# A later input load and held second-layer steps at the start of the deformable layers

## The chip, the cores and the metric

The kernel runs on one core of a Trainium2 chip. The metric is the device time of one execution in microseconds, as the median of runs: 5149.69 us, of three runs between 5146.34 and 5154.36 us. A separate execution was taken by the hardware profiler; all durations in this document come from such executions.

The core has five engines that follow their own lists of instructions in order: TensorE (PE in the profile), VectorE (DVE), ScalarE (ACT), GpSimd (POOL) and SyncE (SP). They wait for each other by semaphores only. POOL and SP also issue DMA transfers, each on a queue of its own.

## The reference, cut to what matters

Four layers follow each other on an input of 2 images, 256 channels, 64 x 64 pixels, in float32:

```python
x = group_norm(x) + proj(attention(group_norm(x)))   # layer 0: four heads over 4096 pixels
x = x + position_term                                # layer 1
h = relu(bn(conv1x1(x)))                             # layer 2: 256 -> 64 channels
h = relu(bn(deform_conv(h)))                         #   3x3 taps, offsets and masks from h
x = relu(bn(conv1x1(h)) + x)                         #   64 -> 256 channels
h = deform_conv(relu(group_norm(x)))                 # layer 3: two deformable 3x3 convolutions
x = deform_conv(relu(group_norm(h))) + x             #   of 256 channels, offsets from h
```

A deformable convolution reads, for each output pixel and each of its nine taps, four neighbouring pixels at an address that was computed from the data, weights them, and multiplies the sum with the weights of the tap:

```python
samp = gather(y0, x0) * w00 + gather(y0, x0+1) * w01 + gather(y0+1, x0) * w10 + gather(y0+1, x0+1) * w11
out = einsum('bckhw,ock->bohw', samp, w)
```

## The kernel before, in words

The program has two functions that follow each other. `attention` computes layers 0 and 1 and, between the products of the attention, layer 2 of the first image and the beginning of the rest. `deform` computes what is left: layer 2 of the second image, and layer 3 of both.

**An image in memory.** Before it is sampled, an image is written to memory by pixels, two rows side by side, so that one row of it holds two neighbouring pixels of two lines, and two such rows, read as one, hold the four neighbours of a sample. A gather (`gather`, line 844) is an indirect DMA on POOL's queue: 128 addresses, one for each partition, from a table of indices in SBUF.

**The main loop of `deform`.** Layer 3 has four passes: two convolutions of two images. Each pass has eight blocks of 512 pixels, each block nine taps of four groups of 128 pixels. A sample `s` is one tap of one group: 36 samples in a block (`BLOCK`), 288 in a pass, 1152 in all. The loop runs over `s` and writes, for each `s`, one turn of a software pipeline:

- `gather(s + 8)`: the four corners of a later sample (tile `four`, 512 KB, ten buffers). `AHEAD` is 8.
- `first(s + 1)`: ScalarE multiplies corner 0 with its weight (L1459).
- `others(s)`: VectorE adds the three other corners, three instructions (L1465).
- `evacuate`, `product`, `turn`: ScalarE copies four turned samples out of PSUM (L1486), TensorE multiplies them with the tap's weights (L1496), and turns sample `s - 2` (two transposes, L1477).

The four engines named take their instructions in exactly the order in which the program writes them; SP's are ordered by the planner.

**Kept samples.** For the first two blocks of the first pass (`EARLY` is 2, so 72 samples) the gathers were already made during the attention, and their results lie in memory (`samp_d`). For these, `gather(s)` is a plain load: on POOL's queue for the first eight, on SP's for the others. From sample 72 on it is an indirect gather on POOL.

**Side work.** Beside the pipeline, further sequences of steps run in small pieces. An object `Side` holds such a sequence, and `follow(s)` runs steps of it as long as their count is below `rate * (s - start) + more(s)`. Three of them matter here:

- `last`: the offsets of the last two blocks of layer 2, second image; one step for each `s`.
- `seconds`: all the sampling of layer 2 for the second image (`conv`, line 1041). Its first seven steps issue one gather of look-ahead each. After that there are 144 units of two steps. The first step of unit n issues gather unit n + 7 and writes the weighting of unit n (VectorE, L1065). The second writes its adds (VectorE, L1075 and L1076) and, now and then, the later parts: transposes, two small products, and the output of a block (L1121, L1127, L1128). A gather unit is two indirect DMAs of 128 KB (tile `bfour`, eight buffers); 288 such DMAs in all.
- `offs`: the offsets of the next block of layer 3 from the input `x`, by products over `x` (L803); for the first pass it starts at sample 14, with block 2.

When `seconds` is at its end, its buffers are given back, and the image of the second pass is made in steps (`image`), beginning with its statistics (L149).

**The input `x`.** `load` (line 1325) brings the input of a pass for one image into SBUF: 256 x 4096 values, 4 MB, in four DMAs; for the first image on POOL's queue (L1331), for the second on SP's. In the kernel before, it is written before the loop, after the first eight kept samples, the nine tiles of weights and the small filter tables.

**Order on POOL.** POOL therefore has at the start of `deform`: eight kept samples alternating with weights, a ninth tile of weights, two filter tables, four pieces of `x`, and then the gathers of `seconds`, each with the semaphores that its buffer needs. POOL's DMAs take turns on eight semaphores, so each DMA waits until the eighth before it has landed.

Of the kernel before, what the change touches and what calls it, by code (L numbers as in the profile page):

```python
# [29 lines left out]
EARLY = 2  # L30
# [34 lines left out]
class Net:  # L65
# [1233 lines left out]
    def deform(self, bott):  # L1299
# [5 lines left out]
        with ExitStack() as ctx:  # L1305
            gp = ctx.enter_context(tc.tile_pool(name="df_g", bufs=10))
            wp = ctx.enter_context(tc.tile_pool(name="df_w", bufs=1))
# [17 lines left out]
            def load(b, src, pool):  # L1325
                x[b] = pool.tile([P, 2, HW], F32, name=f"x{b}")
                src = src.rearrange("(cb p) n -> p cb n", p=P)
                for i in range(4):
                    cols = slice(1024 * i, 1024 * i + 1024)
                    queue = (nc.gpsimd, nc.sync)[b]  # L1330
                    queue.dma_start(x[b][:, :, cols], src[:, :, cols])  # L1331
# [69 lines left out]
            def offsets(b, l):  # L1401
                if b == 0:
                    yield from offset_weights(l)
                wf = self.wf
                for i in range(EARLY if (b, l) == (0, 0) else 0, NB):
                    idx = cp.tile([P, 4, K2], I32, name="didx")
                    w4 = cp.tile([P, 4, K2, 4], F32, name="dw4")
                    corners[b, l, i] = idx, w4
                    yield from self.offsets(
                        i,  # L1410
                        [x[b][:, cb, :] for cb in range(2)],
                        lambda s, row: wf[:, s, DWK * row : DWK * row + DWK, :].rearrange(
                            "p t o -> p (t o)"
                        ),
                        self.vec[:, V_PWB + l : V_PWB + l + 1],
                        base, idx, w4, work, ods[i % 2], pd,
                    )
# [6 lines left out]
            BLOCK = 4 * K2  # L1424
# [10 lines left out]
            def gather(s):  # L1435
                if s < ALL:
                    n, i, k, j = parts(s)
                    b, l = layers[n]
                    fours[s] = gp.tile([P, 4, C], F32, name="four")
                    four = fours[s].rearrange("p s c -> p (s c)")  # L1440
                    if n == 0 and i < EARLY:

                        queue = nc.gpsimd if s < AHEAD else nc.sync
                        m = 4 * k + j
                        queue.dma_start(four, self.samp_d[i][m * P : m * P + P, :])
                        return
                    idx = corners[b, l, i][0]
                    self.gather(four, self.img3[b], idx[:, j, k : k + 1])
# [6 lines left out]
            def first(s):  # L1455

                if s < ALL:
                    smps[s] = sp.tile([P, C], F32, name="smp")
                    nc.scalar.mul(smps[s], fours[s][:, 0], weight(s, 0))  # L1459

            def others(s):
                if s < ALL:
                    four = fours.pop(s)
                    for c in range(1, 4):
                        nc.vector.scalar_tensor_tensor(  # L1465
                            smps[s], four[:, c], weight(s, c), smps[s], ALU.mult, ALU.add
                        )

            def turn(s):

                if 0 <= s < ALL:
                    u, j = divmod(s, 4)
                    if j == 0:
                        pts[u] = ptp.tile([P, 2, 512], F32, name="pt")
                    smp = smps.pop(s)
                    for c in range(2):
                        nc.tensor.transpose(  # L1477
                            pts[u][:, c, j * P : (j + 1) * P],
                            smp[:, c * P : c * P + P],
                            self.ident,  # L1480
                        )

            def evacuate(u):
                if 0 <= 4 * u < ALL:
                    sts[u] = tp.tile([P, 2, 512], F32, name="st")
                    nc.scalar.copy(sts[u], pts.pop(u))  # L1486

            def product(u, q, s):

                if not 0 <= 4 * u < ALL:  # L1490
                    return
                n, i, k, _ = parts(4 * u)
                ob, c = divmod(q, 2)
                if k == 0 and c == 0:
                    outs[ob] = pop.tile([P, 512], F32, name=f"out{ob}")
                nc.tensor.matmul(  # L1496
                    outs[ob],
                    lhsT=wc[k][:, c, ob * P : ob * P + P],
                    rhs=sts[u][:, c, :],
                    start=(k == 0 and c == 0),  # L1500
                    stop=(k == K2 - 1 and c == 1),
                )
                if q == 3:
                    del sts[u]
                    if n == 1 and i == NB - 1:
                        conv_weight(1, k)
                if k == K2 - 1 and c == 1:
                    finish(n, i, ob, s)
# [45 lines left out]
            second = bott.conv(1, bott.pools(inner, 8), ps)  # L1554
# [3 lines left out]
            conv_weight(0, AHEAD)  # L1558
            begun = offsets(0, 0)
            next(begun)  # L1560
            load(0, self.xn_d[0], wp)
            offs = [Side(EARLY * BLOCK - LEAD - 6, OFFS / BLOCK, begun)]
            first(0)


            last = Side(0, 1, bott.last(1, bott.kept, ps))
            seconds = Side(0, 0.9, second, lambda s: 2.5 * min(s, EARLY * BLOCK))
            stats[0] = self.norm_stats()
            images = []
            for s in range(ALL + 12):  # L1570
                n = s // LAYER
                if s == LAYER:
                    stats[1] = self.norm_stats()
                gather(s + AHEAD)
                first(s + 1)
                others(s)
                if (s - 6) % 4 == 0:
                    evacuate((s - 6) // 4)
                product(*divmod(s - 7, 4), s)
                turn(s - 2)  # L1580
                for f in due.pop(s, ()):
                    f()
                last.follow(s)
                if seconds:
                    seconds.follow(s)
                    if not seconds.steps:
                        seconds = None
                        stats[1] = bott.stats[1]
                        inner.close()
                        images.append(Side(s, 0.9, image(*layers[1])))  # L1590
                if s % LAYER == LAYER // 2 and 1 <= n < len(layers) - 1:
                    images.append(
                        Side(s, IMAGE / (LAYER // 2 - LEAD - 12), image(*layers[n + 1]))
                    )
                if s % LAYER == LAYER - LEAD - 8 and n + 1 < len(layers):
                    for o in images + offs:
                        for _ in o.steps or ():
                            pass
                    images, offs = [], []
                    offs.append(Side(s, OFFS / BLOCK, offsets(*layers[n + 1])))  # L1600
                for o in images + offs:
                    o.follow(s)
# [101 lines left out]
```

## Time and profile before

| what | us |
|---|---|
| median of three runs | 5149.69 |
| profiled execution, span | 5149.0 |
| TensorE busy | 4816.8 (94%) |
| VectorE busy | 4196.7 (82%) |
| ScalarE busy | 2883.6 (56%) |
| POOL busy | 2254.7 (44%) |

The profiled execution's own time is its span from the first to the last instruction; the median of the runs lies 0.7 us above it. The mean granted TensorE clock is 0.976 of full speed. `deform` begins at about 2976 us, when POOL clears its first buffers, so that some 2173 us of the span belong to it.

In the slices of the page a digit is the busy share of an engine in tenths, over 128.7 us. A row of the groups gives source line, engine, operation, the tile written and the tiles read, the count, busy time and mean duration, and then the idle time of the engine just before these instructions, with what ended it. A releaser that the profile names is the one that came last by its records; where several semaphores were waited for, another may have been meant. In the rows of the timeline the first two numbers are the start and the duration, and the bracket holds the idle time before the row.

### The profile page before, as it was taken

The numbers are of one execution on the slowest core, as the hardware profiler recorded it, in microseconds if no ns is written. First come the engines' busy times: TensorE is split into PE (matmuls) and PEld (weight loads), VectorE is DVE, ScalarE is ACT, GpSimd is POOL, SyncE is SP. The second block draws the span as 40 slices with busy tenths as digits, with TensorE's granted clock in tenths as the row PEclk, the third lists the DMA queues.
The fourth block names the chain that finished last, engine by engine and source line by source line (L and its number), as shares of the span: only waits on it lengthen the run. The fifth ranks groups of instructions, "written<-read, shape, count | busy, mean of one in ns | idle before, by whom it ended". The sixth has DMA issues, their size and how long they took to land. (4 is left out here: it accounts for less than half of the span.)

```text
span 5149.0 us, 100000 instructions
## 1 busy us (share of the span) xinstructions
PE 4816.8 (94%) x38200; PEld 2651.9 (52%) x38200; DVE 4196.7 (82%) x7929; ACT 2883.6 (56%) x5221; POOL 2254.7 (44%) x2256
## 2 busy tenths in 40 slices
PE   8999999999999999999999957679999999999998
PEld 5555565555565555565555523234444444444443
DVE  6878867878668888687766768878999999999998
ACT  5666656666666666666656622235444554454444
POOL 0111111111107777464023257775666566666665
PEclk9999999999999999999999967789999999999999
DMA  5231121111113333322557677679999999999998
GB/s 172 61 99 51 42 68 49 35 46 30 55 52 94 93 100 102 94 85 79 150 193 272 233 242 239 207 251 376 340 329 339 360 359 350 356 388 346 347 348 318
DMA packets 367022, 997.66 MB, mean 194 GB/s; under 512 B 61372, under 2 KB 98810, under 8 KB 366542
## 3 DMA queue, kind: packets, MB, share of 16 engines
q0 software_dynamic: 196560, 690.41, 37.7%
q1 hardware_dynamic: 169438, 300.73, 17.9%
q8 instruction: 300, 4.92, 0.4%
q14 instruction: 180, 1.47, 0.1%
q10 hardware_dynamic: 544, 0.13, 0.0%
HBM read 855.36 MB, written 127.35 MB: 191 GB/s over the span
## 5 line engine op out<-in xcount | busy, mean ns | idle before, releaser
L1465 DVE SCALAR_TENSOR_TENSOR smp<-four,dw,smp 128x256 f32<-128x256 f32 x3240 | 1503.8, 483 | 122.3 <-ACT smp L1459 44.4
L598 ACT ACTIVATE e<-sc,low 128x1024 f32<-128x1024 f32 x1024 | 1147.1, 1120 | 745.1 <-DVE low L592 741.4
L592 DVE TENSOR_REDUCE low<-sc 128x1 f32<-128x1024 f32 x1024 | 1204.8, 1218 | 228.1 <-PE sc L580 224.0
L846 POOL DMA_INDIRECT four<-img,didx x1080 | 1085.4, 1005 | 646.3 <-DVE smp L1465 349.2
L1496 PE MATMUL out<-st,wc 128*128 128x512 f32 x2304 | 1229.6, 616 | 65.0 <-ACT st L1486 33.6
L580 PE MATMUL sc<-k,qs 64*128 64x512 f32 x2048 | 997.1, 605 | 1.8 <-ACT e L598 1.4
L639 PE MATMUL av<-et,v 128*64 128x256 f32 x8192 | 996.5, 385 | 0.0
L580 PE MATMUL sc<-k,q 64*128 64x512 f32 x2048 | 977.3, 604 | 0.0
L519 POOL TENSOR_TENSOR o<-o,f 128x1024 f32<-128x1024 f32 x63 | 149.3, 2370 | 1771.5 <-DMA f<-share_d 890.1
L610 PEld LDWEIGHTS tt<-ident,e 64*128 64x128 f32 x16384 | 651.7, 139 | 519.3 <-issue 275.4
L1459 ACT ACTIVATE smp<-four,dw 128x256 f32<-128x256 f32 x1080 | 535.9, 507 | 594.3 <-PE pt L1477 460.4
L610 PE MATMUL tt<-ident,e 64*128 64x64 f32 x16384 | 726.1, 226 | 40.5 <-ACT et L629 19.9
L629 ACT COPY et<-tt 128x512 f32<-128x512 f32 x1152 | 659.5, 586 | 170.5 <-PE tt L610 169.2
L627 DVE COPY et<-tt 128x512 f32<-128x512 f32 x896 | 612.0, 683 | 161.3 <-PE tt L610 160.9
L639 PEld LDWEIGHTS av<-et,v 128*64 128x64 f32 x8192 | 552.1, 137 | 302.9 <-issue 48.4
L1477 PEld LDWEIGHTS pt<-ident,smp 128*128 128x128 f32 x2304 | 320.5, 144 | 740.8 <-issue 423.4
L846 POOL DMA_INDIRECT bfour<-img,bidx x576 | 581.0, 1009 | 184.2 <-issue 90.3
L1496 PEld LDWEIGHTS out<-st,wc 128*128 128x128 f32 x2304 | 392.0, 196 | 323.3 <-issue 216.5
L1477 PE MATMUL pt<-ident,smp 128*128 128x128 f32 x2304 | 454.6, 280 | 72.7 <-DVE smp L1465 67.1
L580 PEld LDWEIGHTS sc<-k,qs 64*128 64x128 f32 x2048 | 345.4, 188 | 215.7 <-issue 120.0
L1486 ACT COPY st<-pt 128x1024 f32<-128x1024 f32 x288 | 291.2, 1011 | 289.5 <-PE pt L1477 287.8
L803 PE MATMUL pd<-x,wf 128*126 128x512 f32 x840 | 433.4, 598 | 0.0
(183 smaller groups left out, 3600.4 us busy)
## 6 DMA issues: line engine op xcount, KB each, us to landing
f<-share_d SPq DMA_DIRECT2D x128, 256.0 KB
four<-samp_d SPq DMA_DIRECT2D x64, 512.0 KB
xb<-xn SPq DMA_DIRECT2D x55, 512.0 KB
img<-imgt SPq DMA_DIRECT2D x96, 256.0 KB
four<-img,didx POOLq DMA_INDIRECT x1080, 6.1
xa<-res SPq DMA_DIRECT2D x32, 512.0 KB
samp_d<-xb SPq DMA_DIRECT2D x32, 512.0 KB
xb<-in_x SPq DMA_DIRECT2D x20, 512.0 KB
```

The costliest lines, as they stand in the source:

```text
L580: nc.tensor.matmul(s[:, j, :], lhsT=q[u, i // 2][int(h != j)][halves[j], at : at + P], rhs=k[u][c][halves[j], h, :], start=True, stop=True,)
L592: nc.vector.tensor_reduce(low, s, AX.X, ALU.max, negate=True)
L598: nc.scalar.activation(e.rearrange("p j n -> p (j n)"), s, AF.Exp, bias=blk.low[:, g, c : c + 1], accum_out=blk.sum[:, g, c : c + 1],)
L610: nc.tensor.transpose(pt[:, m, :], e[half, m // 4, m % 4 * P : m % 4 * P + P], self.ident[half, half],)
L627: nc.vector.tensor_copy(dst, pt)
L629: nc.scalar.copy(dst, pt)
L639: nc.tensor.matmul(now["av"][halves[h], :], lhsT=v[u][c][:, m, halves[h]], rhs=ets[j][:, m, h, :], start=(m == 0), stop=(m == 7),)
L846: self.nc.gpsimd.indirect_dma_start(out=dst, out_offset=None, in_=img, in_offset=bass.IndirectOffsetOnAxis(ap=idx, axis=0),)
L1459: nc.scalar.mul(smps[s], fours[s][:, 0], weight(s, 0))
L1465: nc.vector.scalar_tensor_tensor(smps[s], four[:, c], weight(s, c), smps[s], ALU.mult, ALU.add)
L1477: nc.tensor.transpose(pts[u][:, c, j * P : (j + 1) * P], smp[:, c * P : c * P + P], self.ident,)
L1496: nc.tensor.matmul(outs[ob], lhsT=wc[k][:, c, ob * P : ob * P + P], rhs=sts[u][:, c, :], start=(k == 0 and c == 0), stop=(k == K2 - 1 and ...
```

## The change

The load of `x` for the first image is taken from its place before the loop and written in the loop's turn `s == 4`, after that turn's pipeline work and before its side work. The rate of `seconds` is written anew: eight steps are allowed from the start, none more until sample 14, from then 4.4 for each sample until sample 72, and 0.9 for each sample after that. Before, it was 3.4 for each sample until sample 72, and then 0.9.

```diff
             conv_weight(0, AHEAD)
             begun = offsets(0, 0)
             next(begun)
-            load(0, self.xn_d[0], wp)
             offs = [Side(EARLY * BLOCK - LEAD - 6, OFFS / BLOCK, begun)]
             first(0)
 
             last = Side(0, 1, bott.last(1, bott.kept, ps))
-            seconds = Side(0, 0.9, second, lambda s: 2.5 * min(s, EARLY * BLOCK))
+            HELD = 14
+            seconds = Side(
+                0, 0, second,
+                lambda s: 8 + 4.4 * max(0, min(s, EARLY * BLOCK) - HELD)
+                + 0.9 * max(0, s - EARLY * BLOCK),
+            )
             stats[0] = self.norm_stats()
             images = []
             for s in range(ALL + 12):
...
                 for f in due.pop(s, ()):
                     f()
+                if s == 4:
+                    load(0, self.xn_d[0], wp)
                 last.follow(s)
                 if seconds:
                     seconds.follow(s)
```

In the order of POOL's instructions this puts 16 gathers of `seconds` in front of the four pieces of `x`. In VectorE's order the first weighting of `seconds` stands behind sample 0, where it stood behind sample 3, and its first adds stand behind sample 15. The last gather of `seconds` has 27 gathers of layer 3 before it, where it had 48. The number of instructions of each kind is the same.

## The prediction

> **What bounds the kernel now.** I read the page's slices first, because they show where the kernel is not at its steady pace.
>
> ```profile
> PE   8999999999999999999999957679999999999998
> DVE  6878867878668888687766768878999999999998
> POOL 0111111111107777464023257775666566666665
> PEclk9999999999999999999999967789999999999999
> ```
>
> Each slice is 128.7 us. From slice 27 (about 3500 us) to the end TensorE and VectorE are at 9 and the clock is full; before slice 24 (3000 us) the attention keeps TensorE at 9. Between, for four slices, nothing is at 9, and POOL is at its highest. The change is in this stretch, so I cut it into windows: first gathers, gather stretch, its tail, and one steady block of 36 samples for comparison.
>
> ```profile
> 3004.00:3033.00 29.00, 5.04 (x13) 2.53 (x13) 12.06 (x32) 3.16 (x6) 17.15 (x17) 0.50 0.80 291
> 3033.00:3459.00 426.00, 293.44 (x919) 136.66 (x918) 366.69 (x845) 110.91 (x200) 329.10 (x319) 0.80 0.71 227
> 3459.00:3507.00 48.00, 36.92 (x123) 17.03 (x121) 39.90 (x98) 17.96 (x32) 27.36 (x28) 0.89 0.84 308
> 3754.00:3811.00 57.00, 55.07 (x195) 25.99 (x194) 52.76 (x125) 28.23 (x49) 35.70 (x36) 1.00 0.92 330
> ```
>
> The columns are length, busy time of PE, weight loads, DVE, ACT, POOL, granted clock, DMA share, GB/s. In the second row POOL issues 319 gathers in 426 us, 1.335 us each, although it is "busy" for only 329 us. The groups of POOL's lines say what the rest is:
>
> ```profile
> L846 POOL DMA_INDIRECT bfour<-img,bidx x273 | 281.1, 1030 | 83.2 <-issue 45.1 <-DVE smp L1465 11.6 <-DVE bfour L1065 8.5
> L846 POOL DMA_INDIRECT four<-img,didx x48 | 50.5, 1052 | 14.6 <-issue 9.8 <-DMA four<-img,didx 1.5 <-ACT smp L1459 1.5
> ```
>
> (83.2 + 14.6)/321 = 0.30 us of idle before each gather, the same whatever releaser is named. Waits for an engine would vary; a constant gap is the cost of the next issue. So POOL is saturated from 3033 to 3481 us while VectorE has 59 us of slack (366.7 of 426). From then on VectorE and TensorE set the pace: the same piece of the chain, "PE pd L823 x13", starts at 3756.37 and 3813.65, so a steady block of 36 samples takes 57.28 us, 1.59 us each.
>
> The start, in order of time, POOL first and then VectorE:
>
> ```profile
> 2998.80 0.71 POOL L1331 DMA_DIRECT2D x<-xn  x1 [0.77 <-DMA four<-samp_d]
> 3004.22 1.04 POOL L846 DMA_INDIRECT bfour<-img,bidx  x1 [4.72 <-PE pt L1477]
> ...
> 3015.71 0.95 POOL L846 DMA_INDIRECT bfour<-img,bidx  x1 [4.10 <-DMA x<-xn]
> 3019.86 0.94 POOL L846 DMA_INDIRECT bfour<-img,bidx  x1 [3.20 <-DMA x<-xn]
> ...
> 3032.57 0.95 POOL L846 DMA_INDIRECT bfour<-img,bidx  x1 [0.30 <-DVE floor L756]
> ```
>
> ```profile
> 3003.51 0.18 DVE L741 TENSOR_SCALAR mask<-pm 128x36 f32<-128x36 f32 x1
> 3020.28 0.69 DVE L1065 TENSOR_TENSOR bfour<-bfour,bw 128x512 f32<-128x512 f32 x1 [16.59 <-DMA bfour<-img,bidx]
> ```
>
> VectorE stands for 16.59 us, because the first gather (issued 3004.22) lies behind the 4 MB x load on POOL's queue; two later gathers wait 7.3 us for x pieces. The gather at 3032.57 is the 17th: its buffer is the first one reused.
>
> **The change part by part.** Nothing is removed: the second layer has 288 gathers before and after, x is four loads of 1 MB, and the kept samples are 72. Two things move.
>
> *The load.* Its four issues go behind 16 gathers. The gathers then meet a queue without 4 MB in front: I take the other transfer time of such gathers, a median of 3.8 us to landing. The Trainium skill ("DMA: Bandwidth & Descriptors", Anatomy of one DMA) fits 2.0 us plus bytes over 436 GB/s: 128 KB would give 2.3 us as an estimate, 1.5 us earlier. The trace's 3.8 us decides. The first gather must still wait for the last image stores (issued at 2991.6 to 2993); the "PE" in its row is a late semaphore, not a product that it needs. It can issue between 2998 (stores land sooner without the load beside them) and 3004.2; I take 3002, nearer to the row. The load is issued near 3002 + 16 x 1.335 = 3023, and lands by about 3043 (in the trace 3019.9 for issues at 2995 to 2999, 20 us). It is needed by the offsets of block 2, whose products now come at sample 20, near 3060: covered, and if it were late those products would hold TensorE by that lateness.
>
> *The hold.* Eight steps are now let through at sample 0, and then none until sample 15. The eighth step contains the first weighting (L1065), so it stands in VectorE's order right after sample 0, done at 2997.5. Behind it in VectorE's order are samples 1 to 15 and the last two blocks' offset steps; TensorE's transposes wait for those. The first two gathers land at 3002 + 1.3 + 3.8 = 3007.1: a stall of 9.6 us instead of 16.6. Then 0.7 us of weighting, 15 samples at 1.49 us (22.4) and 6.9 us of offset steps (rows of 0.2 to 0.7 us) give 3037. TensorE at half clock adds a wait or two: I take 3039 for the first adds, and 3039.5 for gather 17, which waits for them. Before it was 3032.6. So POOL, which decides, is **7 us later** (0 if the stores land early and nothing waits; 12 if the PE waits add 3 and the load's pieces hold gathers 21 to 24 for 2). Its 7.3 us of waits for x are now covered by the wait for VectorE. SP's queue is not passed by the load; it only carries the second layer's block stores and loads closer together (every 8 kept samples instead of 10 or 11). A store waits for VectorE's output and holds the kept samples behind it, but those are fetched 8 samples ahead: 15 us or more at the new pace, longer than the output's 3.8 us of work, so I charge nothing; without that lead it would be up to 3.8 us for each of 8 blocks.
>
> *The new mix.* From sample 15 to 72 there are 4.4 steps a sample instead of 3.4, so 4.4 gathers: 5.87 us of POOL. VectorE needs 1.46 + 2.2 x 1.61 (weighting 0.69, adds 0.42 and 0.29, a 1/18 share of 3.8 us of output work) + 0.2 = 5.2 us: POOL still bounds. In the two instruction orders 48 block-2 gathers lie before the last second-layer gather before, 27 after. That last gather is number 336 before (3459.4) and 315 after, so after it falls at 3039.5 + 298 x 1.335 = 3437.3: 21 x 1.335 = **28.0 us less** of POOL. But the 21 samples are not gone: they follow at VectorE's and TensorE's pace, 21 x 1.59 = **33.4 us more**. And VectorE enters the end of the gather stretch from a mix with fewer samples per gather; at 2.54 us of POOL against 2.35 us of VectorE per sample (samples 72 to 92) it makes up only part of its way, and I charge 1.5 samples, **2.4 us** (0 to 5).
>
> A second rule is weighed on those 21 samples. "TensorE: Matmul & The Clock Gate" (What's actually happening) has only two clock states, half after an idle window and full when busy. At half clock a product is 0.96 and two transposes 0.63 us (rows near 3057), with offsets about 2.2 us a sample: 46 us for the 21. The row of the tail has 0.89 granted, which by that rule is 22% cold, 36 us. Since POOL then no longer starves TensorE, I take the steady row's 33.4 us and keep 36 for the range.
>
> Sum: +7 - 28.0 + 33.4 + 2.4 = **+14.8 us** on the profiled 5149.0 us, 5163.8; its median of runs is 5149.7, so **5164 us**. From sample 136 on both programs have the same work left, and the next layer's image is only 20 samples earlier with much room, so the shift reaches the end undiminished.
>
> **Rivals.** (a) *No measurable change* (under 0.2%, 10.3 us, about what the runs can tell): gather 17 comes at 3033 and VectorE keeps its lead: -28.0 + 33.4 = +5, 5155 us. For it: the first gathers meet a free queue. Against: fifteen samples stand between them and the release of the first buffer.
>
> (b) *Faster*: VectorE, not POOL, bounds the stretch, so its stall is what counts. If the first gather issues at 2998, the data is there at 3003.1, the stall is 5.6 instead of 16.6 us, and 11.0 us are won: 5139 us. It decides if the stall is below 6.3 us and the saving survives the stretch. For it: the rule of the same DMA page that descriptors cost little to generate, by which 321 issues would be nearly free. Against: the row, 1.335 us each, and 14% idle time of VectorE while POOL has none.
>
> (c) *Clearly slower*: the tail runs cold (46 instead of 33.4 us) or the offset products meet a late x; with the 12 us end of the start, +12 - 28 + 46 + 2 = +32, 5182 us.
>
> **How the numbers follow.** My forecast has 0.45, (a) 0.28, (b) 0.12, (c) 0.15. The forecast's own range is 5157 to 5172; a part of it, about 0.03, lies under 5160. So slower by over 0.2% has 0.57, within 0.2% 0.31, faster 0.12. The range for 8 in 10 goes from 5143, leaving out most of (b), to 5180, leaving out the far half of (c).
>
> **What would show it.** Right: a VectorE wait of 7 to 11 us on L1065 right after the first sample; gather 17 near 3039; POOL at 1.33 us a gather until about 3437; then some 21 more samples before the next image's first statistics (3507 before, near 3521 after). Wrong: gather 17 before 3033; POOL idle inside the stretch with VectorE full; a changed mean of the gathers (0.05 us less would be 15 us); or a tail whose samples take less than 1.5 or more than 1.8 us.

## The result and the profile after

The changed kernel takes **5159.9 us** (median of 13 runs, 5156.9 to 5166.0), the kernel before 5150.9 us beside it: the medians lie 9.0 us apart. The ratio over the runs is 1.0020, with a 95% interval of 1.0013 to 1.0027, that is 6.7 to 13.9 us slower. The forecast was 5164 us on 5149.7, 14.3 us slower, with a range of 5143 to 5180. The sign and the range held; the forecast was 1.6 times the difference of the medians. That difference lies right at the 0.2% (10.3 us) that the prediction named as the bound of what can be told apart. The interval leaves out a difference of zero, but the measured time stands about midway between the forecast and rival (a), which said +5 us. So the time alone does not decide between these two; the steps of the traces, below, do.

POOL's timeline in the profile of the changed kernel (start, duration, then in the bracket the idle time before the row):

```profile
2973.83 1.06 POOL L1421 MEMSET wide<- 128x560 f32 x2 [27.67 <-PE av L639]
...
2999.38 1.02 POOL L846 DMA_INDIRECT bfour<-img,bidx  x1 [7.37 <-DMA four<-samp_d]
...
3019.89 2.95 POOL L1331 DMA_DIRECT2D x<-xn  x4
3034.69 1.22 POOL L846 DMA_INDIRECT bfour<-img,bidx  x1 [11.85 <-DVE bsmp L1076]
...
3045.22 1.13 POOL L846 DMA_INDIRECT bfour<-img,bidx  x1 [1.33 <-DMA x<-xn]
...
3434.38 0.95 POOL L846 DMA_INDIRECT bfour<-img,bidx  x1 [0.30 <-issue]
```

The first row is where `deform` begins on POOL. In the profile of before the same row stands at 2976.17; the attention ahead of it has the same instructions in both, and its end differs by 2.3 us from one execution to the other. So times of this part are given below from that row on. The other rows are gather 1, the moved load, gather 17 (after 11.85 us in which POOL waits for VectorE's first adds), gather 24 (1.33 us for the last piece of `x`), and the last second-layer gather.

VectorE's timeline at the same place has the stall that the prediction put behind sample 0, and the first adds 29.4 us after it:

```profile
2993.48 1.53 DVE L1465 SCALAR_TENSOR_TENSOR smp<-four,bw,smp 128x256 f32<-128x256 f32 x3 [4.04 <-DMA four<-samp_d]
3004.28 0.69 DVE L1065 TENSOR_TENSOR bfour<-bfour,bw 128x512 f32<-128x512 f32 x1 [9.27 <-DMA bfour<-img,bidx]
3004.89 1.52 DVE L1465 SCALAR_TENSOR_TENSOR smp<-four,bw,smp 128x256 f32<-128x256 f32 x3
...
3033.66 0.42 DVE L1075 TENSOR_TENSOR bfour<-bfour 128x256 f32<-128x256 f32 x1
```

The windows of the changed kernel (length, PE, weight loads, DVE, ACT, POOL, clock, DMA share, GB/s) for start, gather stretch, tail and steady block:

```profile
3004.00:3033.00 29.00, 22.71 (x72) 11.45 (x72) 26.26 (x72) 13.14 (x25) 15.18 (x17) 0.76 0.90 324
3033.00:3436.00 403.00, 249.84 (x747) 113.74 (x747) 331.00 (x755) 87.23 (x158) 309.19 (x300) 0.75 0.66 211
3436.00:3507.00 71.00, 61.72 (x223) 30.41 (x222) 60.42 (x150) 32.27 (x56) 39.38 (x39) 0.90 0.92 347
3754.00:3811.00 57.00, 55.06 (x195) 26.06 (x194) 52.72 (x126) 28.26 (x49) 35.63 (x37) 1.00 0.92 331
```

The start looks far better: VectorE is busy for 26.26 of 29 us instead of 12.06, TensorE for 22.71 instead of 5.04. It did not make the kernel faster. In the gather stretch VectorE is now busy 82% of the time instead of 86%: the kept samples that used to be spread over it were partly done at the start, and VectorE waits for gathers more than twice as long. These are its waits for them from 3100 to 3380 us (total, times, longest, in us), in the kernel before and in the changed one:

```profile
DVE bfour L1065 <- DMA bfour<-img,bidx: 17.6, 18, 2.6
DVE bfour L1065 <- DMA bfour<-img,bidx: 41.0, 36, 3.8
```

That is where the gain at the start went. POOL has no such waits. Its gathers in the same 280 us of the changed kernel:

```profile
L846 POOL DMA_INDIRECT bfour<-img,bidx x204 | 208.4, 1022 | 62.1 <-issue 37.2 <-DVE smp L1465 8.5 <-DVE bfour L1065 5.8
```

The 62.1 us of idle time are 0.30 us for each of 204 gathers. Gather 26 serves as a mark below, because no piece of `x` holds a gather behind it. Behind it, up to the last gather of the second layer, there are 310 gathers in the kernel before and 289 in the changed one, and before each of them POOL is idle for 0.30 to 0.31 us, never longer.

The last row of the windows is unchanged work, and the chain of the changed kernel repeats there every 57.2 to 57.3 us as before, 7.9 us later on the clock of the span (before: 3756.37 and 3813.65):

```profile
3764.25 1.88 PE pd L823 x13
3821.53 1.88 PE pd L823 x13
```

Between the gather stretch and this steady block lies the image of the second pass. It begins with the statistics of L149, when the second layer is at its end. Before, and then changed (the first row of before is samples 135 and 136, the last row of changed is 136 and 137, by the count of L1465, which has three instructions for each sample):

```profile
3504.08 2.95 DVE L1465 SCALAR_TENSOR_TENSOR smp<-four,dw,smp 128x256 f32<-128x256 f32 x6
3506.95 0.59 DVE L149 BATCH_NORM_AGGREGATE gn_mv<-gn_stats 128x2 f32<-128x48 f32 x2
```

```profile
3481.11 0.59 DVE L149 BATCH_NORM_AGGREGATE gn_mv<-gn_stats 128x2 f32<-128x48 f32 x2
...
3518.99 3.01 DVE L1465 SCALAR_TENSOR_TENSOR smp<-four,dw,smp 128x256 f32<-128x256 f32 x6
```

All on one scale, in us from the first row of POOL's timeline:

| | before | changed | difference |
|---|---|---|---|
| gather 1 | 28.05 | 25.55 | -2.5 |
| gather 17 | 56.40 | 60.86 | +4.5 |
| last second-layer gather | 483.24 | 460.55 | -22.7 |
| sample 136 | 529.3 | 545.2 | +15.8 |
| steady block ("PE pd L823") | 780.2 | 790.4 | +10.2 |
| end of the span | 2172.8 | 2184.3 | +11.5 |

From sample 200 to beyond sample 450 the difference stands at 10.2 us. Another 1.2 us come in the second pass, where both kernels have the same work. With the 2.3 us that the attention ended sooner in this execution, the spans differ by 9.1 us.

### The profile page after: what moved, and what is told of

The parts are those of the page before. It is cut to its first block, busy times and chain, and to the rows that moved or that the text cites. A ratio compares the mean times of both kernels' runs of the same rounds, so it can differ in the third digit from the quotient of the medians.

```text
span 5158.1 us, 100069 instructions
## 1 busy us (share of the span) xinstructions
PE 4823.4 (94%) x38200; PEld 2654.9 (51%) x38200; DVE 4198.3 (81%) x7929; ACT 2881.4 (56%) x5221; POOL 2254.8 (44%) x2256
## 5 line engine op out<-in xcount | busy, mean ns | idle before, releaser
L1465 DVE SCALAR_TENSOR_TENSOR smp<-four,dw,smp 128x256 f32<-128x256 f32 x3240 | 1502.8, 483 | 112.9 <-ACT smp L1459 35.2
```

The costliest lines, as they stand in the source:

```text
L1465: nc.vector.scalar_tensor_tensor(smps[s], four[:, c], weight(s, c), smps[s], ALU.mult, ALU.add)
```

## Experiments

Two theories were held against each other. *POOL*: the issue of gathers is the bound from gather 17 on, so only what delays POOL, or moves samples out of its stretch, counts. *VectorE*: its work and its stalls are the bound, so the first wait counts. All comparisons are with runs of the kernel before on the same chip. Some of the runs fell on two chips on which the kernel before itself takes 5345 and 5305 us; apart from the second pad for POOL they are told at the end. Two marks serve in all of them: gather 26, as above, and the row "PE pd L823 x13" of the steady block, behind which all kernels have the same work. Both are given in us from the start of the part.

**1. The load alone, without the hold** (start at sample 4, old rate).

```diff
-            load(0, self.xn_d[0], wp)
...
+                if s == 4:
+                    load(0, self.xn_d[0], wp)
```

> The load alone moved, a third time, for a chip on which POOL is saturated: there 3 us faster than before if POOL is the bound (gather 26 at 65.5 us after the start of this part instead of 68.7), 12 us faster if VectorE's first wait counts. On a chip like the first two: no difference, as there.

Measured: 5147.2 beside 5149.2 us, ratio 0.9997 (0.9989 to 1.0006), -1.5 us (-5.7 to +3.1). The theory of POOL (-3) lies inside, that of VectorE (-12) outside. By the trace the steady block comes 2.9 us sooner than before. VectorE's wait did shrink, from 16.59 to 5.18 us, as its timeline shows, and POOL's timeline shows why that is worth so little: the pieces of `x`, now behind 18 gathers, hold later ones for 1.88 + 2.27 + 1.19 us instead of 7.3, and cost 2.94 us of issue that stood ahead of the gathers before.

```profile
3004.29 0.69 DVE L1065 TENSOR_TENSOR bfour<-bfour,bw 128x512 f32<-128x512 f32 x1 [5.18 <-DMA bfour<-img,bidx]
```

```profile
3020.45 2.94 POOL L1331 DMA_DIRECT2D x<-xn  x4
...
3031.72 0.94 POOL L846 DMA_INDIRECT bfour<-img,bidx  x1 [1.88 <-DMA x<-xn]
3034.93 0.94 POOL L846 DMA_INDIRECT bfour<-img,bidx  x1 [2.27 <-DMA x<-xn]
3037.07 0.94 POOL L846 DMA_INDIRECT bfour<-img,bidx  x1 [1.19 <-DMA x<-xn]
```

The last of these rows, gather 26, stands 65.6 us after the start of the part, 68.7 before: the 3 us that were expected.

**2. The hold without VectorE's stall** (seven steps instead of eight).

```diff
-                lambda s: 8 + 4.4 * max(0, min(s, EARLY * BLOCK) - HELD)
+                lambda s: 7 + 4.4 * max(0, min(s, EARLY * BLOCK) - HELD)
```

> The changed kernel with seven steps let through, again: VectorE's wait of 9.3 us is gone, but gather 26 comes only about 3 us sooner (71.5 us after the start in the first trace, 74.2 in the changed kernel). If POOL is the bound: 3 us less than the changed kernel, 6 us more than before. If VectorE's wait counts: 9 us less, equal to before.

Measured: 5156.4 beside 5149.2 us, ratio 1.0014 (1.0007 to 1.0021), +7.2 us. VectorE has no wait on its first weighting at all, and gather 17 comes at 51.8 us instead of 60.9. But gather 26 comes only at 72.8 instead of 74.2, for gathers between 17 and 22 now wait for the pieces of `x` and, by the names in the profile, for VectorE. The first weighting and three of these gathers:

```profile
3021.43 0.68 DVE L1065 TENSOR_TENSOR bfour<-bfour,bw 128x512 f32<-128x512 f32 x1
```

```profile
3030.77 1.06 POOL L846 DMA_INDIRECT bfour<-img,bidx  x1 [3.35 <-DMA x<-xn]
3035.11 0.95 POOL L846 DMA_INDIRECT bfour<-img,bidx  x1 [3.28 <-DVE bfour L1065]
3038.04 0.94 POOL L846 DMA_INDIRECT bfour<-img,bidx  x1 [1.99 <-DMA x<-xn]
```

The theory of POOL said +6, that of VectorE 0, which the interval leaves out; the steady block comes 4.7 us later than before. Taking away 11.4 us of VectorE's stall in experiment 1 moved the steady block by 2.9 us, the 3.1 us of gather 26. Taking away all 9.3 us in experiment 2 moved it by 5.5 us against the changed kernel in these two profiles, where gather 26 gives 1.4; some 4 us of that stay open. By the medians over before, 9.0 and 7.3 us, it is about 2 us.

**3. More work for VectorE in the stretch.** One more instruction after each of samples 16 to 71, whose result nobody reads.

```diff
                             smps[s], four[:, c], weight(s, c), smps[s], ALU.mult, ALU.add
                         )
+                    if 16 <= s < EARLY * BLOCK:
+                        nc.vector.scalar_tensor_tensor(
+                            four[:, 3], four[:, 3], weight(s, 3), smps[s], ALU.mult, ALU.add
+                        )
```

> The changed kernel with one more VectorE instruction of the size of a corner (0.48 us) after each of the samples 16 to 71: 56 more, 27 us of VectorE inside the gather stretch; its result is used by nobody. If POOL is the bound: VectorE has 5.2 us of work beside 5.87 us of POOL per sample, the pad fills the gap, 0 to 6 us more than the changed kernel. If VectorE is the bound: 27 us more.

Measured: 5161.4 beside 5148.6 us, ratio 1.0025 (1.0015 to 1.0035). The changed kernel has 1.0020 on its own, so the 27 us cost some 3 us, which is inside the intervals; in the profile the steady block comes 5.9 us later than in the changed kernel. Both are in the 0 to 6 us of POOL's theory, and far from 27. The work was there: the window 3033 to 3434 has 330.5 us of VectorE in the changed kernel and 351.6 here. It filled VectorE's waits for gathers, which fall from 41.0 us in the changed kernel to 17.6 (3100 to 3380 us):

```profile
DVE bfour L1065 <- DMA bfour<-img,bidx: 17.6, 17, 2.4
```

```profile
3033.00:3434.00 401.00, 244.03 (x728) 110.53 (x728) 351.56 (x800) 85.00 (x155) 309.06 (x295) 0.76 0.65 209
```

**4. More work for POOL in the stretch.** A small fill, which nobody reads, before each of 136 gather pairs, in the changed kernel.

```diff
                     fours[n] = pools["g"].tile([P, 2, 4, CM], F32, name="bfour")
+                    if b == 1 and n >= 8:
+                        nc.gpsimd.memset(net.spare, 0.0)
...
+            self.spare = wp.tile([P, 64], F32, name="spare")
```

> The changed kernel with one small fill (128x64) on POOL before each of 136 gather pairs of the stretch, which nobody uses. If POOL is the bound: the stretch grows by all of it, 136 times the fill's time with its gap, an estimated 0.2 to 0.5 us: 27 to 68 us more than the changed kernel. If VectorE is the bound: less than 10 us more.

Measured: 5161.5 beside 5148.6 us, ratio 1.0025 (1.0015 to 1.0034). By the number that was expected the theory of POOL fails; by the trace the experiment did not test it. The fills ran in the gap that stands between two gathers anyway:

```profile
3200.26 1.12 POOL L846 DMA_INDIRECT bfour<-img,bidx  x1 [0.30 <-issue]
3201.38 0.17 POOL L1057 MEMSET spare<- 128x64 f32 x1
3201.71 1.00 POOL L846 DMA_INDIRECT bfour<-img,bidx  x1 [0.16 <-DVE bfour L1077]
```

From the end of one gather to the next it is 0.33 us with the fill and 0.30 without: 136 x 0.03 = 4 us, and from gather 26 to the last one the stretch did take 390.5 us instead of 386.3. So the pad was repeated with four fills in place of one:

```diff
-                        nc.gpsimd.memset(net.spare, 0.0)
+                        for _ in range(4):
+                            nc.gpsimd.memset(net.spare, 0.0)
```

> The changed kernel with four small fills on POOL before each of 136 gather pairs. One fill took 0.17 us and lay inside the gap between two gathers (0.33 with its own gap, in place of 0.30); three more should add 0.51 us to a pair. If POOL is the bound: 136 x 0.54 = 73 us more than the changed kernel, 5233. If VectorE is the bound (86% busy in the stretch before, 82% after): at most 10 us more, 5170.

Measured, on a slower chip: 5387.0 beside 5305.3 us, ratio 1.0156 (1.0136 to 1.0176), 82 us slower than the kernel before; the forecast of POOL's theory was 73 us over the changed kernel, that of VectorE at most 10. The changed kernel itself was not run on this chip. The timeline gives a gather pair with fills:

```profile
3303.46 0.80 POOL L1058 MEMSET spare<- 128x64 f32 x4
3304.81 0.95 POOL L846 DMA_INDIRECT bfour<-img,bidx  x1 [0.55 <-DVE bsmp L1079]
3306.07 0.94 POOL L846 DMA_INDIRECT bfour<-img,bidx  x1 [0.30 <-issue]
3307.00 0.80 POOL L1058 MEMSET spare<- 128x64 f32 x4
```

One pair takes 3.54 us, 0.8 to 0.9 more than twice 1.337. So 136 pairs hold some 115 us more of POOL, where the forecast had counted 73. That 82 us of them reached the end, close to 73 and the changed kernel's own 9, rests on chance, for two errors cancel: the pad was larger than forecast, and a part of it was absorbed. In this kernel POOL is almost without pause: of its 289 gaps from gather 26 to the last gather only four are over 0.6 us, while the load-alone kernel on the same chip has waits of up to 10.6 us there. So the run shows that POOL's time reaches the end once POOL is the bound; it does not show that POOL was the bound without the fills. Four fills on an ordinary chip were not run.

**5. The rate alone, without the hold** (load at sample 4, 4.4 steps for each sample from the start).

```diff
-            HELD = 14
             seconds = Side(
                 0, 0, second,
-                lambda s: 8 + 4.4 * max(0, min(s, EARLY * BLOCK) - HELD)
-                + 0.9 * max(0, s - EARLY * BLOCK),
+                lambda s: 4.4 * min(s, EARLY * BLOCK) + 0.9 * max(0, s - EARLY * BLOCK),
             )
```

> The load moved, no hold, 4.4 steps for each sample from the start: no gather of layer 3 then lies before the last one of layer 2, where it was 48 before. By my steps: 48 x 1.335 = 64 us less of POOL, 48 x 1.59 = 76 us more after it, 2 to 5 us of lag, and the start of the moved load (-1 to +4): 14 to 22 us over before, 5165 to 5173. If the rate doesn't matter: like the moved load alone.

Measured: 5160.6 beside 5148.6 us, ratio 1.0023 (1.0016 to 1.0030), +12 us (8 to 15). The 12 us lie under the 14 to 22 us expected, though the interval reaches into them. The start is better than before by 7 us at gather 26 (61.5 instead of 68.7), but only one gather of layer 3 lies before the last second-layer one: that comes 69.1 us sooner, and from it to the steady block it takes 76.1 us longer. At sample 136 this kernel is 19.8 us behind, inside the 14 to 22; by the steady block only 7.0 of these are left. The likely reason is the image of the second pass, which began at sample 71 here and was over by sample 136.

**6. The other way** (load at sample 4 on SP's queue; 3.0 steps for each sample until 72, 0.8 after).

```diff
-                lambda s: 8 + 4.4 * max(0, min(s, EARLY * BLOCK) - HELD)
-                + 0.9 * max(0, s - EARLY * BLOCK),
+                lambda s: 3.0 * min(s, EARLY * BLOCK) + 0.8 * max(0, s - EARLY * BLOCK),
...
-                    queue = (nc.gpsimd, nc.sync)[b]
+                    queue = nc.sync
```

> The load on SP at sample 4, and 3.0 steps a sample until 72, 0.8 after: about 90 gathers of layer 3 then lie before the last one of layer 2. By my steps against the load on SP with the old rate: 42 x 1.335 = 56 us more of POOL, 42 x 1.59 = 67 us less after it, so up to 11 us faster, 5131, if POOL stays the bound; POOL and VectorE are then within 3% of each other, and if they wait for each other in turn the gain is eaten, 5141.

Measured: 5146.4 beside 5148.6 us, ratio 0.9992 (0.9984 to 1.0001). Not told apart from before. 88 gathers of layer 3 lie before the last second-layer one, 40 more; that one comes 53.4 us later, and from it to the steady block it takes 55.4 us less. The gain of up to 11 us over the load on SP, 5131, did not come, and the trace shows three reasons. Gather 1 came only at 31.6 us (28.0 before), and gather 26 at 64.0, where 59 had been expected for a load on SP. A sample taken into the stretch saved 1.39 us after it, not 1.59. And a gather took 1.350 us instead of 1.337, which is 4.6 us over 350 gathers; POOL did not wait for VectorE here either, all its gaps are 0.30 to 0.31 us.

The runs on the ordinary chips on one scale (gathers of layer 3 before the last second-layer gather; us from the start of the part to gather 26 and to that last gather; us of POOL for one gather between these two; us from the start to sample 136, to the steady block and to the end of the span):

| kernel | layer-3 gathers before | gather 26 | last | one gather | sample 136 | steady block | end |
|---|---|---|---|---|---|---|---|
| before | 48 | 68.7 | 483.2 | 1.337 | 529.3 | 780.2 | 2172.8 |
| changed | 27 | 74.2 | 460.5 | 1.337 | 545.2 | 790.4 | 2184.3 |
| 1: load alone | 48 | 65.6 | 480.5 | 1.338 | 526.4 | 777.3 | 2174.7 |
| 2: seven steps | 28 | 72.8 | 459.4 | 1.333 | 539.0 | 784.9 | 2180.7 |
| 3: VectorE pad | 27 | 73.8 | 464.1 | 1.350 | 548.7 | 796.3 | 2190.2 |
| 4: one fill | 27 | 73.8 | 464.3 | 1.351 | 547.5 | 792.9 | 2186.2 |
| 5: 4.4, no hold | 1 | 61.5 | 414.1 | 1.341 | 549.1 | 787.2 | 2184.2 |
| 6: 3.0, load on SP | 88 | 64.0 | 536.7 | 1.350 | 486.0 | 778.2 | 2170.9 |

The column "one gather" is the strongest evidence for the theory of POOL: with 4.4 or 3.0 steps a sample, with 27 us more for VectorE, with or without a stall, one gather takes 1.33 to 1.35 us, and POOL is idle for 0.30 to 0.31 us before it, except where experiment 4 has its fills and at three gathers of experiment 5 (the longest gap 2.25 us). The profile's chain alone would not have shown it, for in the kernel before more than half of it runs through VectorE from 3040 to 3240 us. From the last gather to the steady block lies the other half: the samples moved behind the stretch cost 32.9/21 = 1.57, 28.5/20 = 1.43 and 76.1/47 = 1.62 us each (changed kernel, experiments 2 and 5), more than the 1.34 us that POOL saves. Behind the steady block single profiles scatter: with the same work there the changed kernel loses 1.2 us to the kernel before, the load alone 4.8 us and experiment 6 nothing; why was not found out.

**The slower chips.** On the two other chips the kernel before takes 3.0 and 3.8% longer, and the stretch shows another picture. The load alone, on the first of them:

> The load alone is moved behind sample 4 (18 gathers then stand before it on POOL); the steps keep the rate of before. If POOL's issue is the bound: the first gather comes 2.5 us sooner, but the four pieces of x still cost POOL 3 us and hold the gathers that follow them on the same semaphores for 7 to 10 us, as before: within -1 to +4 us of before, 5150 to 5155. If VectorE is the bound: its wait on the first gather shrinks from 16.6 to about 3 us, so 13 us faster than before, near 5138.

5334.6 beside 5345.2 us, ratio 0.9982 (0.9972 to 0.9992): 5 to 15 us faster. That is what the theory of VectorE had said (13), and outside the -1 to +4 of POOL's. The same kernel on the other slow chip:

> The load alone moved, the steps at the rate of before, once more: on the first chip ScalarE and TensorE had waits of up to 25 us that no engine's work explains, and POOL was not saturated there. Gather 26 came at 65.7 us after the start of this part in that trace, 68.7 in the kernel before. If POOL is the bound: 3 us faster than before, 5147 beside 5150. If VectorE is the bound: its first wait falls from 16.6 to 3 to 5 us, 12 us faster, 5138.

5306.6 beside 5305.3 us, ratio 1.0002 (0.9988 to 1.0016): the gain of the first chip is not repeated.

> The hold and the rate of 4.4 alone, the load at its old place. By my steps: the first data lies behind x and comes 44 us after the start of this part, VectorE waits 23 us after sample 0, its 15 samples follow, and gather 17 comes near 74 us instead of 61: 14 us more than the changed kernel, 5174. If the hold itself costs nothing and only the load's place matters: near before, 5151.

The hold and the new rate with the load at its old place, on the first slow chip like the two that follow: 5342.4 beside 5345.2, ratio 1.0001 (0.9989 to 1.0013). Gather 17 came at 69.5 us, not at 74, and the time was not 24 us over before. A miss.

> The changed kernel with seven steps let through instead of eight, so that no weighting stands behind sample 0 and VectorE's wait of 9.3 us is gone; 14 gathers then stand before x. If POOL is the bound: gathers 19 to 22 now wait for the pieces of x, gather 22 comes at about the same 68 us, so the time of the changed kernel within 3 us, 5157 to 5162. If VectorE's wait is what counts: 9 us less, 5151.

5341.3 beside 5345.2, ratio 0.9992 (0.9982 to 1.0002): not told apart from before.

> The load at sample 4 but on SP's queue, the steps at the rate of before. If POOL is the bound: no issue of x and no wait for it on POOL, gather 26 comes near 59 instead of 69 us after the start, about 10 us faster than before, 5141. If the kept samples, which then queue behind x on SP, come late: a wait of VectorE of up to 10 us, which is hidden while POOL is the bound.

5355.2 beside 5345.2, ratio 1.0022 (1.0010 to 1.0033). A miss too; gather 26 came at 64.0 us, not 59.

The waits of the load-alone kernel on the second slow chip (engine and line that waited, what for; total, times, longest, us; "remote" is a wait whose releaser the profile doesn't name), and POOL's gathers in the same 280 us:

```profile
ACT bst L1088 <- remote: 66.4, 5, 19.9
ACT bst L1088 <- PE pm L1086: 65.5, 12, 10.1
POOL bfour L846 <- DVE bsmp L1076: 59.2, 17, 10.6
```

```profile
L846 POOL DMA_INDIRECT bfour<-img,bidx x170 | 174.9, 1029 | 106.4 <-DVE bsmp L1076 59.2 <-issue 40.0 <-DVE bfour L1065 2.1
```

POOL issues 170 gathers there in 280 us, 211 on the ordinary chip, and waits up to 10.6 us for VectorE's adds. That ScalarE's stops of up to 20 us come first, and hold VectorE and then POOL, is read from such lists of waits and not shown by an experiment. POOL is not without pause on those chips, so what follows from that does not carry over to them, and their small differences do not test it. What holds ScalarE there was not found out.

## Why the prediction was right

- *What bounds the stretch.* Right on the ordinary chips, by experiments 1, 2, 3 and 5 and by the gaps of 0.30 us. A POOL that issues without a pause, not an engine with the highest busy share, was the bound; its profile row says 77% busy (329 of 426 us). That the gap is the cost of the next issue holds only in so far as it stands before every gather; POOL is not occupied in it, for experiment 4 put a fill of 0.17 us into it almost for nothing.
- *The rule that descriptors cost little to generate* (the Trainium skill, "DMA: Bandwidth & Descriptors", Anatomy of one DMA). The row was rightly preferred: 1.33 to 1.35 us for every gather in eight kernels.
- *VectorE's wait after sample 0.* Forecast 9.6 us, measured 9.27. Gather 1 was taken at 3002 and came at 25.55 us after the start, 3001.7 on the clock of before.
- *Gather 17: +7 us.* Measured +4.5. VectorE needed 29.4 us from its first weighting to its first adds, where the sum of its rows had 30.0, and the 2 us that I added for waits on TensorE did not occur. The load's pieces held one gather for 1.33 us.
- *21 gathers less: -28.0 us.* Measured between gather 17 and the last: 399.7 instead of 426.8 us, -27.1.
- *21 samples after the stretch: +33.4 and +2.4 us.* Measured from the last gather to the steady block: +32.9. The 21 samples were right to half a microsecond and the lag of 2.4 us did not remain. The other weight for them, half and full clock, was 36 us; the tail had a mean granted clock of 0.90, and no run here tells 33 from 36 us apart by the clock.
- *"The shift reaches the end undiminished".* Wrong. The sum of +14.8 us was for sample 136, and there the changed kernel is 15.8 us behind. But the work left from there on is not the same: the image of the second pass runs beside samples 116 to 170 in the changed kernel and beside 137 to 191 before, so that part of it is done by sample 136. At the steady block 10.2 us are left. That the image's place is the cause is read from the traces: experiment 5, with the image from sample 71 on, gives back 12.8 us after sample 136 in the same way. No run moved the image alone.
- *The sum.* 4.5 - 27.1 + 32.9 = 10.3 us at the steady block against 14.8; the 9.0 us of the medians, and the 11.5 us of this one profile at its end, lie inside the measured interval. Up to sample 136 it was in part luck that the sum fitted: gather 17 came 2.5 us sooner than forecast, and the way from the last gather to sample 136 was 2.7 us longer.
- *A sign that I gave wrongly.* The prediction said that the next image's statistics would come near 3521. They came at 3481.1, sooner than before (3506.9). They follow the end of the second layer, which the change puts behind sample 115 instead of 136; 3521 was right for sample 136 (3519.0). It is the same oversight as in the step before.
- *The rivals.* No change (5155) and the forecast (5164) lie on either side of the measured time, and the traces decide: (a) had gather 17 at 3033, and on the clock of before it came at 3037.0. But (a)'s +5 is about as near to the measured 9.0 as the forecast is, because of the step that was wrong. The faster one rested on VectorE's stall; experiment 1 took most of that stall away and came out at -1.5 us (-5.7 to +3.1), not at -11. For the slower one the samples of the tail would have had to take 2.2 us; they took 1.57.

## What to carry to other kernels

Look at the idle time before each transfer of the engine that issues them: here it was 0.30 us before every gather, so POOL's issue was the bound although it showed 77% busy. Then an idle wait of another engine, even of 16 us and on the profile's chain, was worth almost nothing, and filling it only moved the slack. Work moved out of a stretch is not saved: compare what a unit costs the bound inside the stretch (1.34 us) with what it costs the next bound behind it (1.4 to 1.6 us). When a shift is carried to the end, ask which side work has changed its place meanwhile. And before a pad is used as a test, look whether it fits into a gap.

## What was not expected of the hardware

A fill of 0.17 us on POOL fitted into the 0.30 us between two gathers and cost 0.03 us; the "issue" gap was time in which the engine could execute something else. On two of the chips used the same program took 5305 and 5345 us instead of 5150, with waits of ScalarE of up to 25 us (25.4 in the seven-step kernel) for which the profile names no engine of the core.
